# A two-layer graph attention kernel on one core: where the target's own row joins its early sums

## The chip, the cores and the metric

The kernel runs on one core of a Trainium2 chip. The metric is the device time of one execution in microseconds (us); lower is better. Three runs of the kernel before took 1847.95, 1852.89 and 1860.00 us, median 1852.89. The profile comes from one more execution.

## The reference, cut to what matters

There are 3327 nodes with 1024 features each and a symmetric 0/1 adjacency with self loops on the diagonal (each off-diagonal pair is an edge with a chance of about 0.5%). Two layers follow each other, each of the form `x = layernorm(x + attention(x))`.

```python
# layer 0: 8 heads of 128 features
h = (x @ W).reshape(C, H, D)
e = leaky(alpha_src[:, :, None] + alpha_dst[:, None, :], 0.2)   # per head, target i, source j
attn = softmax(where(adj == 0, -inf, e))
out = einsum('hij,hjd->hid', attn, h)
# layer 1: one head of 1024 features
h = x @ W;  e = leaky(h @ a1 + (h @ a2).T, 0.2)
out = relu(softmax(where(adj > 0, e, -9e15)) @ h)
```

Since exp is monotone, the kernel uses exp(leaky(s+d)) proportional to max(exp(0.8 s) exp(d), exp(0.2 d)) for a target with score s and a source with score d. A softmax is then a weighted sum of source rows over a sum of weights. The edge of a node to itself, its *own* edge, is kept out of the lists of edges and treated apart.

## The kernel before, in words

Rows come in NT = 26 tiles of P = 128 targets. A tile's edges lie in EB + 1 = 5 blocks: blocks 0 and 1 hold sources among the first 13 tiles (NTH = 13), 2 and 3 the rest, each as four groups of 128 source rows for 32 targets each, and block 4 is one group for what did not fit. Matmuls and the weights are fp32.

**Stage 1, projection (0 to about 570 us).** For each tile t, rows of x are loaded, turned by TensorE (L195), multiplied with the weights (`project`, L541, three column cuts of 346 or 347, eight matmuls each), taken out of PSUM by ScalarE (`keep`, L553) and stored to `h0_d` with exp(d) and exp(0.2 d) beside them. Masks of the adjacency are loaded by GpSimd's queue (`load_mask`, L527, three buffers), counted by ScalarE and packed by VectorE (`count`, `words`, L341), then made into edge lists in seven steps a tile (`listing`, L592), whose copies by ScalarE `mvg` (L449) wait for VectorE and GpSimd. The order on every engine is the order in which the program issues. `pace` (L629), called after every second matmul of `project`, moves three generators on: `counts` at every third call, `steps` so that 3/7 of the listing is done when tile 13 begins, and `soon`.

`soon` is `sums_so_far` (L646). It starts at t = 13 and gives, for the first EARLY = 17 targets' tiles, the sums over blocks 0 and 1 while the projection of the later tiles goes on. Per tile: `fetch` gathers four groups of source rows by GpSimd (three buffers, two blocks ahead), `weights` (L674) makes the matrix e on VectorE, `sums` (L686) does 16 matmuls for four heads into a PSUM tile `acc` of two banks, `den` sums the weights, ScalarE copies `acc` out to `z` (L738) and `den` to `dens` (L739), and `z` is stored to `half_d` (L740). There are nine yields a tile. The first matmul into each bank has `start`, so `acc` begins empty. What is left when the projection ends runs in one go (L925).

**Stage 2, layer 0 (about 575 to 1090 us).** `pipeline` (L1322) runs over 26 items `Layer0` (L1059): nine late tiles with five blocks, 17 early ones with blocks 2 to 4. For each, `prepare` (L1069) loads x, the tile's own rows with their two exponentials from `h0_d` (520 KB, `own`), and for an early tile also `half_d` (512 KB, `half`). `own` (L1080) makes the own weights es from `grows`, the loaded exponentials and `loop` (is there a self loop) on VectorE; `scale_own` (L1092) multiplies the own rows with es, eight ScalarE instructions; `sums` adds own (and half) to the accumulators by matmuls with the identity (L1128 to L1133). Gathers of source rows (L1036) use five buffers.

**Stage 3, layer 1 (about 1100 to 1777 us).** 26 items `Target` (L1199): gathers, sums (L1258) and a projection (L1290).

Of the kernel before, what the change touches and what calls it, by code (L numbers as in the profile page):

```python
# [9 lines left out]
F32 = mybir.dt.float32  # L10
# [16 lines left out]
def kernel(  # L27
# [102 lines left out]
    dens = const.tile([P, EARLY, H], F32, name="dens")  # L130
    io_t = const.tile([P, P], F32, name="io_t")

    near = [const.tile([P, NG, HG], F32, name=f"near{b}") for b in range(HB)]

# [377 lines left out]
    with ExitStack() as own, tc.manual_schedule():  # L512
# [14 lines left out]
        def load_mask(t):  # L527
            if t < NT:
                ads[t] = masks[t % 3]
                if t == NT - 1:  # L530
                    nc.vector.memset(ads[t].bitcast(I32), 0)
                    nc.vector.memset(ads[t][:, :1], 1.0)
                for r in pieces(t):
                    nc.gpsimd.dma_start(ads[t][r, :N], adj[at(t, r), :])
# [94 lines left out]
        def pace():  # L629

            slots[0] += 1
            n = slots[0]
            if n % 3 == 0:
                next(counts, None)
            first = 3 * total // 7
            if n <= turn_at[0]:
                aim = 4 + (first - 4) * n / turn_at[0]
            else:
                aim = first + (total - first) * (n - turn_at[0]) / (turn_at[1] - turn_at[0])
            while done[0] < aim:  # L640
                done[0] += 1
                next(steps, None)
            if soon:
                next(soon[0], None)

        def sums_so_far():  # L646
# [39 lines left out]
            def sums(acc, val, b, e, heads_):  # L686
                vals = val[:, :, :D].rearrange("p g (h d) -> p g h d", h=H)
                for h in heads_:
                    for g in range(NG):
                        nc.tensor.matmul(  # L690
                            acc[g * GT : (g + 1) * GT, h // 4, h % 4, :], e[:, g, h, :], vals[:, g, h, :],
                            start=b == 0 and h % 4 == 0, stop=b == HB - 1 and h % 4 == 3,
                        )
# [5 lines left out]

            res = [listed(0), listed(1)]  # L700
            for _ in range(3):
                yield
            for n in range(2):
# [5 lines left out]
            fetch(2)  # L709
            yield  # L710
            yield
            for s in range(EARLY):
                acc = part.bank("L", [P, 2, 4, DH], "part")
                made = []
                for b in range(HB):
                    n = s * HB + b
                    val = src[n % 3]
                    made.append(weights(val, b, res[0], oh))
                    yield
                    if n:  # L720
# [5 lines left out]
                    if b == 0:  # L726
                        yield
                        yield
# [7 lines left out]
                z = part.sbuf("z", [P, 2, 4, DH], 1)  # L736
                for n in range(2):
                    nc.scalar.activation(z[:, n], acc[:, n], AF.Copy)  # L738
                nc.scalar.activation(dens[:, s, :], den, AF.Copy)  # L739
                nc.sync.dma_start(half_d[s], z.rearrange("p n h d -> p (n h d)"))  # L740
# [5 lines left out]
                yield  # L746

# [19 lines left out]
        masks = [pool.tile([P, NP], U8, bufs=1, name=f"ad{n}") for n in range(3)]  # L767
# [107 lines left out]
        for t in range(3, NT):  # L875
# [3 lines left out]
            if t == 12:  # L879
# [11 lines left out]
            if t == 16:  # L891
# [80 lines left out]
    def sparse(own):  # L972
# [7 lines left out]
        grows = pool.tile([P, NT, H], F32, bufs=1, name="grows")  # L980
        nc.scalar.activation(grows, sd0[:, :, 0, :], AF.Exp, scale=1 - SLOPE)
# [77 lines left out]
        class Layer0:  # L1059
# [9 lines left out]
            def prepare(self):  # L1069
# [4 lines left out]
                self.h = sbuf("own", [P, HW0], 2)  # L1074
                nc.sync.dma_start(self.h, h0_d[self.t * P : (self.t + 1) * P, :HW0])
                if self.t < EARLY:
                    self.half = sbuf("xT", [P, KT, P], 2, "half").rearrange("p k q -> p (k q)")
                    nc.sync.dma_start(self.half, half_d[self.t])

            def own(self):  # L1080

                t, h = self.t, self.h
                es, total = sbuf("es0", [P, 2, H], 2).rearrange("p a h -> a p h")
                nc.vector.tensor_tensor(es, grows[:, t, :], h[:, D : D + H], OP.mult)
                nc.vector.tensor_tensor(es, es, h[:, D + H :], OP.max)
                nc.vector.tensor_scalar(es, es, loop[:, t : t + 1], None, op0=OP.mult)
                self.es = self.total = es
                if t < EARLY:
                    self.total = total
                    nc.vector.tensor_tensor(total, es, dens[:, t, :], OP.add)  # L1090

            def scale_own(self):  # L1092

                h = self.h
                for n in range(H):
                    d = slice(n * DH, (n + 1) * DH)
                    nc.scalar.activation(h[:, d], h[:, d], AF.Copy, scale=self.es[:, n : n + 1])  # L1097
# [25 lines left out]
            def sums(self, b):  # L1123
# [4 lines left out]
                if j in (1, 2):  # L1128
                    for rows_ in (self.h, self.half) if self.t < EARLY else (self.h,):
                        nc.tensor.matmul(  # L1130
                            self.acc[j - 1].rearrange("p h d -> p (h d)"), ident, rows_[:, (j - 1) * HALF : j * HALF],
                            start=False, stop=False,
                        )  # L1133
# [32 lines left out]
            def finish(self):  # L1166

                ri = sbuf("ri", [P, H], 2)
                nc.vector.tensor_tensor(ri, self.den, self.total, OP.add)
# [391 lines left out]
```

## Time and profile before

| what | value |
|---|---|
| median of 3 runs (lowest to highest) | 1852.89 us (1847.95 to 1860.00) |
| the profiled execution, its own time | 1778.88 us |
| its span, first to last instruction | 1777.1 us, mean granted TensorE clock 0.926 |
| TensorE busy over the span | 1518.3 us (85%) |
| VectorE, ScalarE, GpSimd busy | 1150.6, 537.5, 1111.7 us |
| moved by DMA | 592.41 MB, mean 333 GB/s |
| own<-h_d, 26 loads | 520.0 KB each |
| half<-half_d, 17 loads | 512.0 KB each |

The profiled execution was 74 us shorter than the median. A time and a difference read from the profile belong to that execution. "PE" is TensorE's matmuls, "PEld" its weight loads, "DVE" VectorE, "ACT" ScalarE, "POOL" GpSimd, "SP" the queue of SyncE, which issues most plain transfers. A wait is put down to the engine or transfer that came last. "DMA share" is the mean busy share of the 16 DMA engines in a window.

### The profile page before, as it was taken

How to read it: one execution, taken by the hardware profiler on the slowest of the kernel's cores; microseconds unless marked ns; L12 is line 12 of the kernel's file. 1: busy time of each engine (PE TensorE's matmuls, PEld its weight loads, DVE VectorE, ACT ScalarE, POOL GpSimd, SP SyncE). 2: the span in 40 equal slices, each digit the busy share in tenths (PEclk: the TensorE clock that was granted, in tenths of full speed). 3: DMA queues.
4: the chain of work that ended last, by engine and by line, in shares of the span. 5: the costliest groups of instructions: out<-in, count | busy, mean ns of one | idle time of the engine just before them, and what ended most of it. 6: DMA issues, size and time to landing. Idle time of an engine off the chain costs nothing.

```text
span 1777.1 us, 36731 instructions
## 1 busy us (share of the span) xinstructions
PE 1518.3 (85%) x13778; PEld 882.2 (50%) x13778; DVE 1150.6 (65%) x3125; ACT 537.5 (30%) x1602; POOL 1111.7 (63%) x1476
## 2 busy tenths in 40 slices
PE   8799999999995667666676674599999999999998
PEld 5466666666664455444554453244444444444443
DVE  6799999888873877767777775243444444444443
ACT  5678773333322233233333332011110111101110
POOL 4443358877755666656656666677676666676750
PEclk9999999999998788888788886899999999999999
DMA  7578978998888999999999999999999999999980
GB/s 195 100 138 167 163 170 302 319 314 319 296 303 331 407 411 408 394 384 406 395 397 393 385 402 365 355 395 403 396 393 386 394 390 396 401 401 395 386 345 36
DMA packets 189050, 592.41 MB, mean 333 GB/s; under 512 B 37069, under 2 KB 47079, under 8 KB 188864
## 3 DMA queue, kind: packets, MB, share of 16 engines
q0 software_dynamic: 131056, 458.88, 72.6%
q1 hardware_dynamic: 57650, 130.84, 19.8%
q8 instruction: 111, 1.82, 0.4%
q14 instruction: 75, 0.61, 0.1%
q10 hardware_dynamic: 158, 0.26, 0.0%
HBM read 590.02 MB, written 53.33 MB: 362 GB/s over the span
## 4 chain that ended last, share of the span: by engine, by line
PE 42%; DMA 18%; DVE 4%; issue 1%; ACT 1%; POOL 1%; DVEq 0%; SPq 0%; POOLq 0%; ACTq 0%
PE mm L1290 21%; PE acc L1258 13%; DMA src<-h_d,idx 7%; DMA own<-h_d 4%; PE acc L1147 3%; DMA near<-h_d,idx 3%; PE acc L1130 3%; DVE e L1115 2%; PE tr L195 1%; DMA src<-y_d,idx 1%; DMA near<-y_d,idx 1%; ACT own L1097 1%; DMA end<-h_d,idx 1%; DVE pr L1002 1%; PE acc L1138 1%
## 5 line engine op out<-in xcount | busy, mean ns | idle before, releaser
L545 PE MATMUL mm<-wt,xT 128*128 128x347 f32 (+1 forms) x1248 | 408.0, 468 | 2.1 <-DMA wt<-in_L_gnn_W_dram 1.5
L1290 PE MATMUL mm<-wt,xT 128*128 128x512 f32 x832 | 387.6, 604 | 0.0
L1036 POOL DMA_INDIRECT src<-y_d,idx x240 | 244.6, 1019 | 95.0 <-issue 32.7
L545 PEld LDWEIGHTS mm<-wt,xT 128*128 128x128 f32 x1248 | 225.7, 192 | 116.7 <-issue 18.4
L1036 POOL DMA_INDIRECT src<-h_d,idx x168 | 180.9, 1077 | 112.4 <-PE acc L1147 25.2
L1290 PEld LDWEIGHTS mm<-wt,xT 128*128 128x128 f32 x832 | 149.7, 189 | 199.1 <-issue 194.1
L1293 DVE SCALAR_TENSOR_TENSOR o<-mm,y 128x512 f32<-128x512 f32 x52 | 36.0, 692 | 317.1 <-PE mm L1290 317.1
L1036 POOL DMA_INDIRECT near<-y_d,idx x176 | 178.9, 1017 | 90.6 <-PE acc L1258 29.7
L1130 PE MATMUL acc<-own,ident 128*128 128x512 f32 x104 | 80.4, 865 | 118.8 <-ACT own L1097 115.2
L1036 POOL DMA_INDIRECT near<-h_d,idx x104 | 116.1, 1117 | 65.1 <-DMA src<-h_d,idx 13.9
L198 ACT ACTIVATE xT<-tr 128x512 f32<-128x512 f32 x104 | 63.2, 609 | 254.1 <-PE tr L195 254.0
L1272 ACT ACTIVATE z<-y,ri 128x342 f32<-128x342 f32 (+1 forms) x78 | 39.5, 569 | 300.5 <-DVE ri L1268 300.5
L660 POOL DMA_INDIRECT near<-h_d,idx x96 | 105.2, 1096 | 36.2 <-issue 24.4
L1120 ACT ACTIVATE w<-way 128x32 f32<-128x32 f32 (+1 forms) x96 | 18.5, 192 | 350.4 <-DVE e L1115 168.6
L1115 DVE TENSOR_TENSOR e<-oh,way 128x1024 f32<-128x1024 f32 x96 | 117.2, 1221 | 8.4 <-DVE way L1113 0.5
L1147 PE MATMUL acc<-src,e 128*32 128x128 f32 x2688 | 103.4, 318 | 17.6 <-DVE e L1115 17.6
L1258 PE MATMUL acc<-src,es 128*32 128x342 f32 (+1 forms) x1440 | 116.2, 454 | 0.2
L1258 PE MATMUL acc<-near,es 128*32 128x342 f32 (+1 forms) x1056 | 90.1, 476 | 28.0 <-DVE es L1249 28.0
L1147 PEld LDWEIGHTS acc<-src,e 128*32 128x32 f32 x2688 | 88.1, 129 | 47.1 <-DVE e L1115 31.9
L1147 PE MATMUL acc<-near,e 128*32 128x128 f32 x1792 | 65.8, 309 | 23.0 <-DVE e L1115 12.2
L348 ACT ACTIVATE junk<-ad 128x1664 uint8<-128x1664 uint8 x52 | 82.9, 1594 | 5.6 <-POOL ad L337 4.0
L1130 PEld LDWEIGHTS acc<-own,ident 128*128 128x128 f32 x104 | 20.4, 245 | 124.6 <-ACT own L1097 123.9
(238 smaller groups left out, 2577.8 us busy)
## 6 DMA issues: line engine op xcount, KB each, us to landing
own<-h_d SPq DMA_DIRECT2D x26, 520.0 KB
y_d<-y SPq DMA_DIRECT2D x26, 514.0 KB
y<-y_d SPq DMA_DIRECT2D x26, 514.0 KB
h_d<-ht SPq DMA_DIRECT2D x25, 520.0 KB
x<-in_x_dram SPq DMA_DIRECT2D x25, 512.0 KB
y<-in_x_dram SPq DMA_DIRECT2D x25, 512.0 KB
out_dram<-o SPq DMA_DIRECT2D x25, 512.0 KB
ad<-in_adj_dram POOLq DMA_DIRECT2D x25, 415.9 KB
```

The costliest lines, as they stand in the source:

```text
L198: nc.scalar.activation(part, tr, AF.Copy)
L348: nc.scalar.activation(junk, ad[:, n * THR : (n + 1) * THR], AF.Copy, accum_out=self.d[:, n : n + 1])
L545: nc.tensor.matmul(acc, xT[t][:, k, :], wt[:, k, CUTS0[c] : CUTS0[c + 1]], start=k == 0, stop=k == KT - 1)
L660: nc.gpsimd.indirect_dma_start(out=src[n % 3][:, g, :], out_offset=None, in_=h0_d[:THR, :], in_offset=bass.IndirectOffsetOnAxis(ap=idx[:, ...
L1036: nc.gpsimd.indirect_dma_start(out=s[:, g, :w], out_offset=None, in_=table[:n, :], in_offset=bass.IndirectOffsetOnAxis(ap=idx[:, t, b * NG ...
L1115: nc.vector.tensor_tensor(e, oh.unsqueeze(2).to_broadcast([P, ng, H, wide]), wp.unsqueeze(3).to_broadcast([P, ng, H, wide]), OP.mult,)
L1130: nc.tensor.matmul(self.acc[j - 1].rearrange("p h d -> p (h d)"), ident, rows_[:, (j - 1) * HALF : j * HALF], start=False, stop=False,)
L1147: nc.tensor.matmul(self.acc[h // 4][g * GT : (g + 1) * GT, h % 4, :], e[:, g, h, :], rowsof[:, g, h, :], start=first and h % 4 == 0, stop= ...
L1258: nc.tensor.matmul(self.acc[c][to, :m], es[:, g, :], s[:, g, CUTS[c] : CUTS[c + 1]], start=b == 0, stop=b == EB,)
L1272: nc.scalar.activation(z[:, cut], self.res[:, cut], AF.Copy, scale=ri[:, 1:2])
L1290: nc.tensor.matmul(acc, xT[:, k, :], wt1[:, k, half], start=k == 0, stop=k == KT - 1)
L1293: nc.vector.scalar_tensor_tensor(o[:, half], acc, 0.0, res[:, half], op0=OP.max, op1=OP.add)
```

## The change

- In `sums_so_far`, before the first sum of a tile, ScalarE writes the tile's own row, scaled by the own weight head by head, into `acc`: `lay` first has TensorE write zeros into a bank (one bf16 matmul of 512 columns with `start`), then ScalarE four times 128 columns. The sums have no `start` any more and so add to that. The row comes from `h0_d` by `own_row`, on SP's queue, into the storage of the masks, all of which must have been counted before (`need(NT - 2)`).
- The copy out of `acc` and its store are split into `settle(s, 0)` and `settle(s, 1)`; the second is issued in the first step of the next tile. The denominator is added to `own_e` by VectorE.
- `own_terms` makes the own weights for many tiles at once from the scores `sd0` (three Exp on ScalarE, three VectorE instructions): tiles 0 to 12 before the sums, 13 to 16 at s = 10, the nine late ones at the start of stage 2. `grows`, `dens`, the per-tile `own` arithmetic are gone.
- In layer 0 an early tile loads only `half_d`, into `own`; it has no scaling and one identity matmul per bank instead of two. A late tile loads 512 instead of 520 KB and scales as before.
- `pace` moves `counts` on at two of five calls instead of one of three, and `steps` so that 2/5 instead of 3/7 of the listing is done at tile 13. Masks rotate by one buffer; the diagonal of the adjacency is loaded at t = 5 instead of 12 and `loop` made at 11 instead of 16.

```diff
+    own_e = const.tile([P, NT, H], F32, name="own_e")
+    def own_terms(lo, hi, mids):
+        e, score = own_e[:, lo:hi, :], sd0[:, lo:hi, 1, :]
+        for mid, scale in zip(mids, (1.0, SLOPE)):
+            nc.scalar.activation(mid, score, AF.Exp, scale=scale)
+        nc.scalar.activation(e, sd0[:, lo:hi, 0, :], AF.Exp, scale=1 - SLOPE)
+        nc.vector.tensor_tensor(e, e, mids[0], OP.mult)
+        nc.vector.tensor_tensor(e, e, mids[1], OP.max)
+        nc.vector.tensor_tensor(e, e, loop[:, lo:hi].unsqueeze(2).to_broadcast([P, hi - lo, H]), OP.mult)
...
-                ads[t] = masks[t % 3]
+                ads[t] = masks[(t + 1) % 3]
...
-            if n % 3 == 0:
+            if n * 2 % 5 < 2:
                 next(counts, None)
-            first = 3 * total // 7
+            first = 2 * total // 5
...
-                            start=b == 0 and h % 4 == 0, stop=b == HB - 1 and h % 4 == 3,
+                            start=False, stop=b == HB - 1 and h % 4 == 3,
...
+            def own_row(s):
+                nc.sync.dma_start(row, h0_d[s * P : (s + 1) * P, :D])
+            def lay(s, n):
+                nc.tensor.matmul(
+                    acc[:, n], zeros, all_b.unsqueeze(1).to_broadcast([P, 4, P]), start=True, stop=False
+                )
+                for h in range(4 * n, 4 * n + 4):
+                    nc.scalar.activation(
+                        acc[:, n, h % 4, :], row[:, h * DH : (h + 1) * DH], AF.Copy, scale=own_e[:, s, h : h + 1]
+                    )
+            def settle(s, n):
+                if n == 0:
+                    zs.append(part.sbuf("z", [P, 2, 4, DH], 1))
+                nc.scalar.activation(zs[s][:, n], acc[:, n], AF.Copy)
+                if n == 1:
+                    nc.vector.tensor_tensor(own_e[:, s, :], own_e[:, s, :], den, OP.add)
+                    nc.sync.dma_start(half_d[s], zs[s].rearrange("p n h d -> p (n h d)"))
+            need(NT - 2)
+            row = ph.ads.rearrange("p a b -> p (a b)").bitcast(F32)[:, :D]
+            acc = part.bank("L", [P, 2, 4, DH], "part")
...
             for s in range(EARLY):
-                acc = part.bank("L", [P, 2, 4, DH], "part")
                 made = []
                 for b in range(HB):
                     n = s * HB + b
                     val = src[n % 3]
                     made.append(weights(val, b, res[0], oh))
+                    if b == 0 and s:
+                        settle(s - 1, 1)
+                        lay(s, 0)
                     yield
+                    if b == 0 and s:
+                        lay(s, 1)
                     if n:
                         fetch(n + 2)
                     yield
...
                     if b == 0:
                         yield
+                        if s + 1 < EARLY:
+                            own_row(s + 1)
...
-                z = part.sbuf("z", [P, 2, 4, DH], 1)
-                for n in range(2):
-                    nc.scalar.activation(z[:, n], acc[:, n], AF.Copy)
-                nc.scalar.activation(dens[:, s, :], den, AF.Copy)
-                nc.sync.dma_start(half_d[s], z.rearrange("p n h d -> p (n h d)"))
+                if s == EARLY - 1:
+                    yield
+                settle(s, 0)
...
             def prepare(self):
-                self.h = sbuf("own", [P, HW0], 2)
-                nc.sync.dma_start(self.h, h0_d[self.t * P : (self.t + 1) * P, :HW0])
-                if self.t < EARLY:
-                    self.half = sbuf("xT", [P, KT, P], 2, "half").rearrange("p k q -> p (k q)")
-                    nc.sync.dma_start(self.half, half_d[self.t])
+                self.h = sbuf("own", [P, D], 2)
+                h0 = h0_d[self.t * P : (self.t + 1) * P, :D]
+                nc.sync.dma_start(self.h, half_d[self.t] if self.t < EARLY else h0)
...
             def scale_own(self):
+                if t >= EARLY:
+                    for n in range(H):
+                        d = slice(n * DH, (n + 1) * DH)
+                        nc.scalar.activation(h[:, d], h[:, d], AF.Copy, scale=own_e[:, t, n : n + 1])
...
-                    for rows_ in (self.h, self.half) if self.t < EARLY else (self.h,):
-                        nc.tensor.matmul(
-                            self.acc[j - 1].rearrange("p h d -> p (h d)"), ident, rows_[:, (j - 1) * HALF : j * HALF],
-                            start=False, stop=False,
-                        )
+                    nc.tensor.matmul(
+                        self.acc[j - 1].rearrange("p h d -> p (h d)"), ident, self.h[:, (j - 1) * HALF : j * HALF],
+                        start=False, stop=False,
+                    )
```

## The prediction

> **What bounds the kernel now.** I read the page's slices first, to see that one number doesn't describe the whole span, then busy times by stretch.
>
> ```profile
> PE   8799999999995667666676674599999999999998
> DMA  7578978998888999999999999999999999999980
> GB/s 195 100 138 167 163 170 302 319 314 319 296 303 331 407 411 408 394 384 406 395 397 393 385 402 365 355 395 403 396 393 386 394 390 396 401 401 395 386 345 36
> ```
>
> ```profile
> core 0: us, PE busy (x) PEld busy (x) DVE busy (x) ACT busy (x) POOL busy (x), PEclk, DMA share, GB/s
> 75.00:252.00 177.00, 172.82 (x782) 113.89 (x780) 158.82 (x451) 137.06 (x385) 72.29 (x260) 1.00 0.85 152
> 252.00:570.00 318.00, 285.33 (x3373) 194.81 (x3372) 251.89 (x676) 109.20 (x412) 229.78 (x386) 0.97 0.88 309
> 575.00:1090.00 515.00, 348.30 (x5565) 252.77 (x5564) 383.48 (x955) 161.68 (x475) 328.32 (x303) 0.80 1.01 395
> 1100.00:1777.00 677.00, 644.24 (x3693) 276.88 (x3693) 291.39 (x867) 79.41 (x164) 435.56 (x429) 0.98 0.94 366
> ```
>
> Columns: stretch, length, busy time of each engine, TensorE's clock, DMA share, rate. The projection is TensorE's twice: 172.8 of 177 us, and with the early sums 285 of 318. Layer 0 belongs to the transfers: share 1.01 throughout, while no engine exceeds 383 of 515 us. Layer 1 is TensorE's and the change leaves it alone. Next, the transfers of layer 0 and its waits:
>
> ```profile
> q0 software_dynamic: 43391, 151.33, 74.8%
> q1 hardware_dynamic: 17317, 51.40, 25.9%
> ```
>
> ```profile
> PEld acc L1130 <- ACT own L1097: 123.9, 25, 14.1
> DVE es L1084 <- DMA own<-h_d: 46.1, 17, 13.2
> ```
>
> Packets, MB and share of 575 to 1090 us; then waits as sum, times, longest. TensorE stands 124 us behind the scaled own rows, a tempting number. But the transfer engines never rest meanwhile, so only removed bytes shorten this stage. Last, TensorE between two tiles of early sums, where the change puts its new work, and two ScalarE groups of 252 to 570 us:
>
> ```profile
> 389.54 0.29 PE L732 MATMUL dd<-w,oh 128*32 128x8 f32 x16
> 389.76 2.60 PE L545 MATMUL mm<-wt,xT 128*128 128x347 f32 x8
> ...
> 392.40 1.42 PE L545 MATMUL mm<-wt,xT 128*128 128x347 f32 x4
> 393.65 0.33 PE L468 MATMUL xp<-mvg,place 128*128 128x168 bf16 x3
> 395.14 1.08 PE L690 MATMUL part<-near,e 128*32 128x128 f32 x32 [1.16 <-issue]
> ```
>
> ```profile
> L449 ACT ACTIVATE mvg<-mvs,own_g 128x129 bf16<-128x129 bf16 x60 | 19.2, 395 | 39.9 <-POOL mvs L332 17.1 <-DVE mvs L438 14.2 <-DVE place L442 4.3
> L738 ACT ACTIVATE z<-part 128x512 f32<-128x512 f32 x34 | 18.5, 600 | 44.2 <-PE dd L732 25.1 <-PE part L690 12.9 <-issue 6.2
> ```
>
> From the end of one tile's denominator (389.8) to the next tile's first sum (395.1) TensorE has 5.3 us, 1.2 idle.
>
> **What the skill says.** The Trainium skill, "PSUM — Partial Sum Buffer", "The four PSUM rules", says that ScalarE's writes don't touch the bits by which a matmul adds or overwrites; hence the zero matmul ahead of each `lay`. Its section "PSUM bank collisions raise a hardware error" asks that accesses by two engines be ordered by bank. The instruction order of the changed kernel goes further, across both banks of the one tile: the second zero matmul of the first tile waits for ScalarE, though ScalarE touched only the other bank; a tile's first sum waits for ScalarE and its second half has no such wait, so the first covers both `lay`s; each of the four copies waits for the previous one. "DMA: Bandwidth & Descriptors", "Issuing engines are not separate DMA queues", says that transfers from SP and GpSimd share 16 engines; the trace agrees, their shares adding to 1.01.
>
> **The change, part by part.** The sum is made against the profiled execution (own time 1778.9, span 1777.1 us). The median is 74 us above it; I add differences to the median unscaled.
>
> *Layer 0, bytes.* 17 own loads of 520.0 KB go: 9.05 MB (KB of 1024 bytes). At 395 GB/s that is 22.9 us; by queue q1's own rate (25.9% of 515 us for 51.40 MB, 2.6 us a MB) 23.5. Nine late tiles save 8 KB each, 0.2 us. **-23 us.**
>
> *Layer 0, engines.* 34 identity matmuls of 0.87 us, 136 ScalarE copies (eight take 2.44 us in the timeline, 41 us in all), and three or four small VectorE instructions a tile (0.17 us each) go. Behind the transfers this is worth nothing; without that cover, 17/26 of the 124 us wait, 81 us, would be its ceiling. Bound from both sides: 0 by the share of 1.01, and if the rate rose to the best slices' 411 GB/s, (203.6 - 9.05)/0.411 = 473 us, 42 less than 515. I take 0 beyond the bytes and keep -42 as the far end.
>
> *Early sums, transfers.* 17 own rows of 512 KB move here on SP's queue, behind x loads, h stores and half stores; 8.9 MB at 2.6 us a MB, 23 us of DMA time. The stretch uses 0.88 of 318 us, 280, and then 303: 0.95. They fit if spread evenly. A row is issued five steps ahead, some 10 us; own rows are waited for up to 13 us in layer 0's full queues. Late rows would stop ScalarE, and behind it the h copies that the projection needs. Between 0 and 15 us; **+2**.
>
> *Early sums, the chain ahead of a tile's first sum.* Two copies out (L738, a pair takes 1.06 to 1.09 us), zero matmul, four copies, zero matmul, four copies. No trace row has ScalarE writing SBUF into PSUM; nearest is L1097, 0.388 us each, 0.305 apart when they overlap. Waiting for each other they don't, so 0.41; four are 1.6 us (bounds: 1.2 overlapped, 2 with slower hand-overs). A zero matmul of 512 bf16 columns: the skill's "TensorE: Matmul & The Clock Gate", "Back-to-back issue gap", states 518 cycles, 0.22 us at the full clock; L468's 168 columns take 0.24 with drain, so 0.25 to 0.3. With four hand-overs of some 0.1 us: 1.1 + 3.2 + 0.5 + 0.3 = 5.1 us. Into the same queue come ScalarE's other copies: (109.2 - 18.5)/318 = 0.29 of the time, 1.4 us; and `mvg` stands between a tile's first copy out and its last `lay` in about six of 17 tiles by the changed order, at 1.3 us plus its share of the 39.9 us waits (2.7 per listed tile, of which I count half): 6 x 2.6/17 = 0.9. Sum 7.4 against 5.3 now, +2.1 on 16 boundaries: 34 us. TensorE is idle 33 of 318 us; a later first sum gives VectorE and gathers time, whose waits (L690 stands 16.8 us behind DVE e, more on the weight loads) shrink; 10 us come back. **+24.** Bounds: +6 (chain in the idle time; bare zero matmuls) and +50 (nothing comes back, chain 8.5).
>
> *Tail.* The last two tiles have little projection to hide behind: the serial chain costs **+2**.
>
> *Stage 1 up to 252 us.* `counts` runs 6/5 as fast, the first-half listing shrinks from 80 to 74 steps. VectorE gets less before tile 13 and some 12 us more after: 252 + 12 of 318, still under TensorE. The transfer share 0.85 rises while masks last. The diagonal's load, 4.7 us on SP at L886, now stands ahead of x loads at t = 5, covered by their lead of three tiles. `own_terms` adds nine Exps in three calls and nine small VectorE instructions, `settle` 17 adds, minus `dens`'s 17 copies: 4 us on engines with room. 0, or up to +6 if a mask is late; the new `need` then stops the program at tile 13.
>
> Sum: -23 + 2 + 24 + 2 = +5 us, **1858 us**.
>
> **Rivals.**
> *The chain is hidden (faster).* For: TensorE's 33 us of idle time; ScalarE is 34% busy. Then stage 1 costs 3 us. Layer 0, with fewer separate loads and no own-row dependency for early tiles, runs at 400 GB/s: 194.6/0.400 = 486, 29 less. -26: **1827 us**. Against: the chain alone is 5.1 of 5.3 us, and in-order queues wait at its places.
> *The chain becomes the bound (slower).* Place: first sum of each tile, behind ScalarE. Price: 4 us a boundary, 64 us, 16 back, -23: +25, **1878 us**. It decides once a boundary grows by more than (23 + 18)/16 = 2.6 us net. For: `mvg`'s waits, reaching 4 us; the wait across both banks.
> *The transfer was hidden anyway.* If layer 0 had kept time by TensorE's own-row waits, losing them would bring more, not less; if by gathers' issue on GpSimd (328 of 515 us busy), nothing: 1853 + 28 = 1881. The share of 1.01 speaks against it.
> *The change doesn't do what it says.* Bytes might merely move between two full stages; the projection's 0.88 speaks against that, and the time would again be about 1876.
>
> **How the numbers follow.** 1% (18.5 us) is about what a measurement of this kernel can tell from no change. Likeliest, 0.46: layer 0 gives 23 and early sums take about as much; own range 1838 to 1871. Hidden chain, 0.24, around 1827: faster by over 1%. Chain, late rows, late masks, or hidden transfers, 0.30 together, around 1878: slower by over 1%. The 8-in-10 range leaves out half of the faster case's far side and the slow one's: 1827 to 1886.
>
> **What would show it.** Layer 0 still at share 1.0 and about 195 MB, shorter by 23 us: right. The stretch from tile 13 to the last half store longer by about 28 us, with TensorE's weight loads or matmuls at the zero matmul and first sum waiting for ScalarE: right; no such waits, the first rival. ScalarE waiting for the own row: transfers too slow. A share much below 1 in layer 0 would upset the byte sum, and a pause at 250 us would put the loss on the masks.

## The result and the profile after

The changed kernel takes 1899.22 us (median of 4 runs, 1897.00 to 1907.72); the kernel before, run beside it, 1851.19 us (1847.95 to 1860.00). The ratio is 1.026, 95% interval 1.021 to 1.031: slower, by about 48 us where 5 were forecast. The profiled execution of the changed kernel took 1900.04 us, with a span of 1898.3 us, so this time the profile and the median agree.

One thing has to be said ahead of all that follows: the chips were met in two conditions. In one the unchanged kernel before takes about 1780 us (the profile shown ahead of the prediction, and experiments e1 to e8), in the other about 1855 us (the three times ahead of the prediction, the comparison above, and e9 to e15). I call them the 1780 and the 1855 condition. The record gives the same chip number for e5 to e8, which met the first, and for e12 to e15, which met the second. So the profile of before shown ahead of the prediction and the profile of after come from different conditions, and a before from each (e1, e9) is needed to read them.

The slices of the page of the kernel after:

```profile
PE   8799998888788568777778877499999999999998
...
GB/s 183 95 135 165 193 219 259 267 287 254 238 293 275 304 376 377 368 319 393 384 336 369 386 361 384 306 359 388 380 387 371 385 375 380 394 390 384 367 360 34
```

Slices 7 to 13, the early sums, show TensorE at 7 to 8 tenths where the earlier profile had mostly 9. Slices 15 to 25, layer 0, show a rate of 319 to 393 GB/s; in the earlier profile layer 0 lies in slices 14 to 24 and has 384 to 411. Now busy time by stretch: first the kernel after in the 1855 condition (the profile of the comparison), then the kernel before in that condition (e9), then the kernel after in the 1780 condition (e5). Columns as in the prediction: stretch, length, busy time of TensorE, its weight loads, VectorE, ScalarE and GpSimd, TensorE's clock, DMA share, GB/s. In each, the first line is the early sums and the second is layer 0.

```profile
252.00:640.00 388.00, 321.46 (x3434) 210.32 (x3435) 267.28 (x735) 159.85 (x559) 221.68 (x403) 0.95 0.79 273
645.00:1195.00 550.00, 419.69 (x5629) 278.93 (x5630) 374.89 (x885) 128.24 (x350) 335.88 (x315) 0.84 0.96 366
```

```profile
252.00:595.00 343.00, 308.38 (x3365) 203.46 (x3363) 254.44 (x684) 111.22 (x421) 220.96 (x386) 0.97 0.81 279
600.00:1158.00 558.00, 427.92 (x5717) 277.29 (x5718) 391.45 (x977) 165.78 (x484) 333.63 (x316) 0.84 0.99 380
```

```profile
252.00:600.00 348.00, 305.38 (x3372) 203.78 (x3370) 267.35 (x737) 160.23 (x565) 222.54 (x401) 0.97 0.84 300
605.00:1110.00 505.00, 325.35 (x5595) 251.57 (x5599) 373.17 (x883) 123.74 (x344) 330.18 (x308) 0.79 1.01 392
```

The reader is to see two things. In the 1780 condition the change did to layer 0 what was forecast: the share stays at 1.01, and the stage takes 505 us where before had 528 there (e1: 568 to 1096 us). In the 1855 condition TensorE is busy in layer 0 for 428 us before and 420 us after, where it needs 352 (e1) and 325 (e5) in the other condition for about the same number of matmuls, and the share falls to 0.96 once the bytes are gone. Transfers are no longer what this stage waits for most. The chain of waits, followed back from the end, says the same: over layer 0 of the kernel before it lies on transfers for more than half of the time in e1 (`src` gathers 25.6%, `near` gathers 12.9%, own rows 12.8%, `end` gathers 4.0%), but in e9 mainly on TensorE's matmuls into the accumulators (L1147 30.7%, L1130 13.5%) and on pauses that the profile puts down to nothing (19.8%). The largest waits of the kernel after in layer 0 (sum, times, longest):

```profile
PEld acc L1190 <- issue: 204.6, 324, 11.7
...
PE acc L1190 <- issue: 96.7, 253, 1.1
```

The wait for the scaled own rows that led this list before (124 us in the profile ahead of the prediction) is gone from the top; in its place stand pauses that the profile puts down to nothing, marked "issue". In the kernel before in the same condition they lead already (e9, the same view; L1147 is the same line there):

```profile
PEld acc L1147 <- issue: 163.7, 252, 11.3
```

In the 1780 condition it is small (e1, 568 to 1096 us):

```profile
PEld acc L1147 <- issue: 20.5, 7, 11.5
```

Last, the place where the prediction put its chain: TensorE between two tiles in the kernel after, and ScalarE beside it. This boundary is one of the short ones, 5.9 us; the mean is 8.8.

```profile
337.13 0.35 PE L787 MATMUL dd<-w,oh 128*32 128x8 f32 x16
...
338.67 0.38 PE L719 MATMUL part<-all_b,zeros 128*128 128x512 bf16 x1
338.89 1.33 PE L555 MATMUL mm<-wt,xT 128*128 128x347 f32 x4
340.72 0.38 PE L719 MATMUL part<-all_b,zeros 128*128 128x512 bf16 x1 [0.50 <-ACT part L723]
340.94 1.33 PE L555 MATMUL mm<-wt,xT 128*128 128x347 f32 x4
343.39 1.08 PE L700 MATMUL part<-far,e 128*32 128x128 f32 x32 [1.13 <-ACT part L723]
```

```profile
337.50 1.09 ACT L730 ACTIVATE z<-part 128x512 f32<-128x512 f32 x2 [2.96 <-issue]
339.09 1.58 ACT L723 ACTIVATE part<-ad,own_e 128x128 f32<-128x128 f32 x4 [0.50 <-PE part L719]
340.61 1.26 ACT L459 ACTIVATE mvg<-mvs,own_g 128x129 bf16<-128x129 bf16 x4
341.78 1.56 ACT L723 ACTIVATE part<-ad,own_e 128x128 f32<-128x128 f32 x4
```

Everything stands in the forecast order: both copies out, zeros, four own copies (1.58 us; 1.6 were forecast), `mvg` in between, zeros, four copies, and only then, at 343.39, the first sum. These are TensorE's waits there over the early sums (252 to 640 us) in the kernel after; in the kernel before (e1, e9) the sums show no wait for the copies out, and ScalarE writes nothing into the accumulators:

```profile
PE part L719 <- ACT z L730: 28.0, 12, 4.7
...
PEld part L700 <- ACT part L723: 24.4, 16, 4.0
...
PE part L700 <- ACT part L723: 14.4, 13, 2.5
```

From the start times of single rows I made a table of stages in us. "Early sums end" is the start of the last copy out of `acc`; "layer 0" runs from there to the start of its last block-4 matmul; "boundary" is the mean over the 16 tile changes of the time from the end of a tile's denominator to the next tile's first sum, as in the prediction.

| run | kernel | condition | early sums end | layer 0 | boundary |
|---|---|---|---|---|---|
| e1 | before | 1780 | 565.9 | 533.2 | 4.6 |
| e5 | after | 1780 | 603.3 | 509.9 | 7.1 |
| e3 | after, two accumulators | 1780 | 575.9 | 508.5 | 5.0 |
| e7 | after, no own row | 1780 | 575.2 | 509.1 | 4.5 |
| e8 | after, own row loaded but unused | 1780 | 575.1 | 508.3 | 4.7 |
| e9 | before | 1855 | 598.2 | 561.8 | 4.7 |
| e15 | after | 1855 | 644.3 | 552.6 | 8.9 |
| e11 | after, two accumulators, two stores | 1855 | 622.3 | 550.6 | 5.9 |
| e12 | before, fewer bytes | 1855 | 602.5 | 552.0 | 4.7 |
| e13 | after, no own row | 1855 | 605.9 | 551.6 | 4.7 |

Layer 1 (first to last projection matmul) takes 622 us in the first condition and 644 to 645 in the second, in both kernels.

### The profile page after: what moved, and what is told of

Read it like the earlier page. It is cut to its first block, busy times and chain, and to the rows that moved or that the text cites. A ratio compares the mean times of both kernels' runs of the same rounds, so it can differ in the third digit from the quotient of the medians.

```text
span 1898.3 us, 36583 instructions
## 1 busy us (share of the span) xinstructions
PE 1635.8 (86%) x13744; PEld 927.4 (49%) x13744; DVE 1136.4 (60%) x3057; ACT 549.1 (29%) x1593; POOL 1089.6 (57%) x1476
## 4 chain that ended last, share of the span: by engine, by line
PE 55%; issue 7%; DVE 2%; DMA 1%; POOL 0%; DVEq 0%; POOLq 0%; ACT 0%; ACTq 0%
PE mm L1333 20%; PE acc L1301 14%; PE acc L1190 12%; PE acc L1181 4%; PE acc L1173 3%; PE tr L205 1%; DVE pr L1056 1%; PE den L1201 1%; DMA av<-in_L_gnn_a_dram 0%; DMA near<-y_d,idx 0%; DMA src<-y_d,idx 0%; PE tr L1237 0%; DVE e L1159 0%; POOL near L1090 0%; PE den L1185 0%
## 5 line engine op out<-in xcount | busy, mean ns | idle before, releaser
L555 PE MATMUL mm<-wt,xT 128*128 128x347 f32 (+1 forms) x1248 | 422.0, 478 | 3.3 <-DMA wt<-in_L_gnn_W_dram 2.9
L555 PEld LDWEIGHTS mm<-wt,xT 128*128 128x128 f32 x1248 | 232.8, 197 | 155.5 <-issue 62.4
L1333 PEld LDWEIGHTS mm<-wt,xT 128*128 128x128 f32 x832 | 149.6, 189 | 200.6 <-issue 195.6
L1190 PE MATMUL acc<-src,e 128*32 128x128 f32 x2688 | 149.4, 295 | 56.9 <-issue 53.2
L1190 PE MATMUL acc<-near,e 128*32 128x128 f32 x1792 | 108.9, 298 | 58.1 <-issue 44.8
L1190 PEld LDWEIGHTS acc<-src,e 128*32 128x32 f32 x2688 | 92.3, 117 | 119.1 <-issue 104.4
L1090 POOL DMA_INDIRECT near<-h_d,idx x104 | 111.3, 1070 | 58.3 <-issue 19.0
L1301 PE MATMUL acc<-src,es 128*32 128x342 f32 (+1 forms) x1440 | 126.4, 455 | 3.5 <-issue 1.8
L670 POOL DMA_INDIRECT near<-h_d,idx x96 | 102.5, 1067 | 43.9 <-issue 24.9
L1301 PE MATMUL acc<-near,es 128*32 128x342 f32 (+1 forms) x1056 | 97.1, 468 | 25.6 <-DVE es L1292 22.5
L1190 PEld LDWEIGHTS acc<-near,e 128*32 128x32 f32 x1792 | 64.6, 117 | 105.8 <-issue 101.4
L1164 ACT ACTIVATE w<-way 128x32 f32<-128x32 f32 (+1 forms) x96 | 18.2, 190 | 268.6 <-DVE e L1159 160.4
L1181 PEld LDWEIGHTS acc<-end,e 128*128 128x128 f32 x416 | 77.2, 279 | 15.9 <-issue 11.4
```

Source lines behind the costliest of these rows:

```text
L555: nc.tensor.matmul(acc, xT[t][:, k, :], wt[:, k, CUTS0[c] : CUTS0[c + 1]], start=k == 0, stop=k == KT - 1)
L670: nc.gpsimd.indirect_dma_start(out=src[n % 3][:, g, :], out_offset=None, in_=h0_d[:THR, :], in_offset=bass.IndirectOffsetOnAxis(ap=idx[:, ...
L1090: nc.gpsimd.indirect_dma_start(out=s[:, g, :w], out_offset=None, in_=table[:n, :], in_offset=bass.IndirectOffsetOnAxis(ap=idx[:, t, b * NG ...
L1181: nc.tensor.matmul(self.acc[h // 4][:, h % 4, :], e[:, 0, h, :], rowsof[:, 0, h, :], start=False, stop=h % 4 == 3,)
L1190: nc.tensor.matmul(self.acc[h // 4][g * GT : (g + 1) * GT, h % 4, :], e[:, g, h, :], rowsof[:, g, h, :], start=first and h % 4 == 0, stop= ...
L1301: nc.tensor.matmul(self.acc[c][to, :m], es[:, g, :], s[:, g, CUTS[c] : CUTS[c + 1]], start=b == 0, stop=b == EB,)
```

## The experiments

My theory after the result: the chain behind ScalarE at each tile change is the loss, and it is as long as it is because both banks are one tile of the program, so that each step waits for the other bank too. The rivals are the store of `z` (one buffer, its second half copied only when the next tile has begun), the own rows' transfers, and that the difference of 48 us is one of chips. The runs of one group below were measured beside one another, and beside the kernel before.

**e1, e2, e3, e4: one group, 1780 condition.** e1 is the kernel before, unchanged.

> The kernel before, unchanged, profiled once more. The profile of the kernel after shows three stretches longer than that of before: the stretch of early sums (252 us to the last copy out of the accumulators) by 78 us, layer 0 not shorter, layer 1 by 23 us, though the change doesn't touch layer 1; its records have pauses before TensorE's weight loads that are put down to nothing ('issue'). Theory A, the execution and not the change made part of this: a second profile of before gives about 1850 us, with early sums ending near 580 us, layer 0 near 540 us long and layer 1 some 20 us longer than in the first, and the pauses are in it. Theory B, the change made all of it: about 1779 us again, with the same stretches as in the first profile and no such pauses.

Measured: 1779.87 us, ratio 0.9987 to the kernel before in the same group (0.9974 to 1.0000; the 95% interval stands in brackets from here on), span 1777.5 us. The profile ahead of the prediction was no accident of one execution: this condition comes back, and holds for a whole group of runs.

e2 gives each half of `z` a buffer and a store of its own (tile 0's turned rows move to make room):

```diff
-                xT[t] = ph.sbuf("xT", [P, KT, P], 2) if t else part.sbuf("z", [P, KT, P], 1, "xT")
+                xT[t] = ph.sbuf("xT", [P, KT, P], 2) if t else far[:, 1, :D].rearrange("p (k q) -> p k q", q=P)
...
-                if n == 0:
-                    zs.append(part.sbuf("z", [P, 2, 4, DH], 1))
-                nc.scalar.activation(zs[s][:, n], acc[:, n], AF.Copy)
+                z = part.sbuf("z", [P, 4, DH], 2)
+                nc.scalar.activation(z, acc[:, n], AF.Copy)
...
-                    nc.sync.dma_start(half_d[s], zs[s].rearrange("p n h d -> p (n h d)"))
+                nc.sync.dma_start(half_d[s][:, n * HALF : (n + 1) * HALF], z.rearrange("p h d -> p (h d)"))
```

> The kernel after, but each half of a tile's early sums is copied out to a buffer of its own (two half buffers in the room of one) and stored at once, so that the first copy of the next tile no longer waits for a store that was issued only one step into that tile. Theory 'store': in the profile of after the copies out wait 30 us for something without a name, 7 times, and the event waits before them have a median of 3.3 us; this is the store of the tile before, and TensorE's 28 us wait for the copies follows from it. Then this runs about 25 to 30 us faster than after, near 1872. Theory 'chain': the order of zero matmul, copies, zero matmul, copies across both banks is what TensorE waits for; then it gains under 8 us, above 1890.

Measured: 1795.35 us, ratio 1.0078 (1.0062 to 1.0095). The kernel after itself has 1.0067 (1.0043 to 1.0090) in this condition (e5), which is the same within the intervals. The theory of the store falls.

e3 makes the two banks two tiles and leaves all else (the places that name `acc` change with it):

```diff
-            part.more_banks(own, "part", {"L": 1})
+            part.more_banks(own, "part", {"L": 2})
...
-            acc = part.bank("L", [P, 2, 4, DH], "part")
+            acc = [part.bank("L", [P, 4, DH], "part") for _ in range(2)]
```

> The kernel after, but the accumulator of the early sums is two tiles of one bank each, so that the second zero matmul doesn't wait for ScalarE's writes to the first bank, and the first sum only for those to its own bank. Theory 'chain': of the some 60 us that TensorE stands in the early sums behind ScalarE (28 behind the copies out, 9 at the zero matmuls and about 24 at the first sums behind the own rows), the last two shrink to a few us: about 25 us faster than after, near 1874. Theory 'store': under 8 us, above 1890.

Measured: 1765.67 us, ratio 0.9915 (0.9893 to 0.9936). The same work, and 30 us less than e2 beside it, which has the kernel after's time. One of its tile changes:

```profile
306.52 0.29 PE L787 MATMUL dd<-w,oh 128*32 128x8 f32 x16
...
308.01 0.38 PE L719 MATMUL part<-all_b,zeros 128*128 128x512 bf16 x1
...
309.40 0.38 PE L719 MATMUL part<-all_b,zeros 128*128 128x512 bf16 x1
...
310.87 1.08 PE L700 MATMUL part<-near,e 128*32 128x128 f32 x32
```

From 306.81 to 310.87, 4.1 us, and no matmul in it shows a wait for ScalarE; over all early sums its row `PEld part L700 <- ACT part L723` falls to 11.7 us (25.9 in e5). So the order by bank that the Trainium skill asks for ("PSUM — Partial Sum Buffer", "PSUM bank collisions raise a hardware error") is enough here, and in this condition the wait across banks was the cost. e4 has both edits:

> Both edits together, two stores and two accumulators. If the two waits are separate, the gains add: some 50 us faster than after, near 1848, about the time before, since layer 0 has lost its bytes but zero matmuls and own copies stay. If the two are one queue seen at two places, it gains no more than the better of the two alone (1872 or so). If it ends clearly under 1840, the bytes saved in layer 0 show.

Measured: 1764.96 us, ratio 0.9902 (0.9882 to 0.9922): the same as e3 within the intervals, and a shorter time than both kernels have in this condition.

**e5, e6, e7, e8: one group, 1780 condition, to take the sum apart.** e5 is the kernel after, unchanged.

> The kernel after, unchanged, beside the kernel before on one chip. The second profile of before showed that the first one was no accident: 1777.5 us, the same stretches; so the chips differ (before took 1851 on one and 1782 on another). Theory 'the change alone': the ratio stays at 1.026, some 1828 us where before takes 1782; layer 0 is about 24 us shorter than before's and layer 1 equal, and the early sums take all of the loss, ending 70 us later than 566. The pauses without a name of the first profile of after (89 us before TensorE's sums in layer 0) are then absent. Rival, the change brings the pauses: they are here again, and layer 0 isn't shorter.

Measured: 1794.21 us, ratio 1.0067 (1.0043 to 1.0090), before 1780.86. e6 is the kernel before in which an early tile loads no own row in layer 0. It also scales nothing and has one identity matmul a bank instead of two there, and so leaves out the early tiles' own edge:

```diff
                 self.h = sbuf("own", [P, HW0], 2)
-                nc.sync.dma_start(self.h, h0_d[self.t * P : (self.t + 1) * P, :HW0])
                 if self.t < EARLY:
-                    self.half = sbuf("xT", [P, KT, P], 2, "half").rearrange("p k q -> p (k q)")
-                    nc.sync.dma_start(self.half, half_d[self.t])
+                    nc.sync.dma_start(self.h[:, :D], half_d[self.t])
+                else:
+                    nc.sync.dma_start(self.h, h0_d[self.t * P : (self.t + 1) * P, :HW0])
...
```

> The kernel before with one edit in layer 0: an early tile loads only its half sums and not its own row, adds only these with one identity matmul per bank, and scales nothing. It leaves out the own edge of the early tiles, in sums and denominators. This is layer 0's part of the change by itself. Theory 'bytes': 9.05 MB at 395 GB/s, 23 us less: ratio 0.987. Theory 'waits': if TensorE's 124 us behind the scaled own rows set the pace, up to 81 us less, ratio 0.955. Theory 'hidden': no change, 1.00.

Measured: 1760.75 us, ratio 0.9874 (0.9844 to 0.9904), 20 us less by the medians of this group, 22 by the ratio, where 23 were forecast for the bytes. The bytes and the work on the engines go together here and weren't told apart; the sum of both is no more than the bytes were to bring. e7 is the kernel after without zeros, own rows and own copies in the early sums, so it leaves out the own edge as well:

```diff
-                            start=False, stop=b == HB - 1 and h % 4 == 3,
+                            start=b == 0 and h % 4 == 0, stop=b == HB - 1 and h % 4 == 3,
...
-            own_row(0)
...
-            lay(0, 0)
...
-                        lay(s, 0)
...
-                        lay(s, 1)
...
-                        if s + 1 < EARLY:
-                            own_row(s + 1)
```

> The kernel after without zero matmuls, own rows and own copies in the early sums; the first sum of a bank starts it, as before. It leaves out the own edge of the early tiles in the sums. Kept are the split copies out, the store that is issued a step later, the pacing and the masks read by tile 12, and layer 0's saving. If these are harmless, it takes the time of the bytes alone (0.987). If the late store and the wait across both banks cost without any own row, it is slower, up to 1.005.

Measured: 1763.22 us, ratio 0.9895 (0.9875 to 0.9915). So splitting the copies out and the new pacing cost 2.5 us over e6, which is within the intervals. e8 is e7 with the own rows loaded and unused (the two `own_row` calls put back):

> As the one before, but the own rows are loaded in the early sums and used by nobody: the price of their transfers alone. The prediction gave 2 us (0 to 15) for them: ratio within 0.002 of the kernel without them. If the transfers of the early sums are as full as their share of 0.88 lets fear, 15 us or 0.008 more.

Measured: 1766.18 us, ratio 0.9908 (0.9886 to 0.9930). The rows cost 3.0 us, again within the intervals. From e8 to e5 are 28.0 us, the chain; e3, which has all of it but the wait across banks, stands at e8's ratio.

**e9, e10, e11: one group, 1855 condition.** e9 is the kernel before, e10 the kernel after, both unchanged, e11 is e4 again.

> The kernel before again, in the hope of a chip like that of the first comparison, where before took 1851 us. There the profile of after has some 70 pauses a 100 us before TensorE's weight loads in layer 0 (40 us in 100, put down to nothing), where the later profile of after has 4, and its chain of waits in layer 0 is TensorE's, not the transfers'. If the chip is of that kind and the pauses are its own, they are in this kernel too, layer 0 takes about 545 us here as well, and TensorE carries it. If they come with the change, they are absent here. If the chip takes 1781 us, this tells nothing new.

> The kernel after on the same chip. On a chip of the first kind: ratio 1.026 as at first, with layer 0 about as long as before's, since where TensorE carries layer 0, fewer bytes save nothing and only 34 identity matmuls go; the early sums then make the loss of some 50 us. On a chip of the second kind: 1.007 again.

> The version with two accumulators and two stores on the same chip. On a chip of the second kind 0.990 again. On one of the first kind the saved bytes don't show and the chain is mended: 0.995 to 1.005.

Measured: e9 1860.24 us, ratio 0.9991 (0.9970 to 1.0011); e10 1895.43 (two runs only, 1887.85 and 1903.01), 1.0196 (1.0134 to 1.0257), before 1861.17; e11 1876.94, 1.0095 (1.0069 to 1.0121). e10 is slower than before, but by less than the 1.026 that I expected, which lies just beyond its interval. e11 missed what I expected of it: the version that gains 1% in one condition loses 1% in the other. Layer 0 gains only 11 us in e11 (550.6 against 561.8) and the early sums end 24 us later, not 7. The wait across banks costs there as well (e11 is 18.5 us below e10), but it isn't all: e13 below, without any own row, has a ratio of 0.9998, so the chain with two tiles, its rows included, still costs about 18 us in this condition (an estimate from the two ratios).

**e12, e13, e14, e15: one group, 1855 condition.** e12 is e6 and e13 is e7 again, e15 the kernel after.

> Before, with early tiles loading only their half sums in layer 0 (it leaves out their own edge in sums and denominators), a second time, in the hope of a chip on which before takes about 1855 us. Theory 'TensorE carries layer 0 there': on such a chip the bytes give what layer 0 gave in the kernel after, 9 to 12 us: 1843 to 1847 of 1855, ratio 0.993 to 0.996. Theory 'bytes are worth as much everywhere, and the kernel after loses them elsewhere': 22 us, ratio 0.988. On a chip on which before takes about 1781 it repeats 0.987.

Measured: 1855.59 us, ratio 0.9986 (0.9971 to 1.0001), before 1857.47. Less than either theory gave: layer 0's part of the change brings 2 us. In the table layer 0 is 10 us shorter than in e9 and the early sums end 4 us later. But e9 is from another group, in which the kernel before took 4 us more, so stages of different groups agree only to some us, and for the whole time the medians of one group decide. That layer 0 itself is 9 to 11 us shorter than e9's holds for e11, e12, e13 and e15 alike; why so little of it is left in e12's time isn't resolved.

> After without zero matmuls, own rows and own copies in the early sums (it leaves out their own edge in the sums), a second time. On a chip on which before takes about 1855 us the early sums of the kernel after end 44 to 50 us later than before's. Theory 'the chain costs more there': nearly all of it goes with the chain, the early sums end within 10 us of before's and the ratio is 0.993 to 1.0. Rival 'splitting the copies out and the new pacing cost there': the early sums still end 20 us or more later, and the ratio is 1.005 or more. On a chip on which before takes about 1781 it repeats 0.99.

Measured: 1855.95 us, ratio 0.9998 (0.9984 to 1.0012). The early sums end at 605.9, 8 us after before's and 38 before those of the kernel after: nearly all of the delay goes with the chain, here too.

e14 asks what TensorE's pauses in layer 0 come from. It is the kernel after, but gathers only one group of four there once a buffer has been filled, so it leaves out the right rows for the other three:

```diff
+            whole = w != HW0 or k not in filled
+            if not end:
+                filled.add(k)
-            for g in range(NG if b < EB else 1):
+            for g in range(NG if b < EB and whole else 1):
```

> After, with three of four gathers of layer 0 left out once each buffer has been filled (sums of layer 0 then use rows that are not theirs). Transfers of layer 0 fall from about 200 to some 85 MB. On a chip of about 1781: if transfers carry layer 0, its stretch falls from 510 us to what TensorE's 325 us and its waits need, 380 to 430 us, time 1680 to 1720. On a chip of about 1855: if TensorE's pauses of 0.3 us come from contention with the transfers, they vanish and layer 0 takes the same 380 to 430 us there; if they are TensorE's own or its instruction supply's, the pauses stay, and layer 0 stays at 520 us or more.

> The kernel after, unchanged, for the same chip as the three others: 1.02 to 1.026 where before takes about 1855 us, 1.007 where it takes about 1781.

Measured: e14 1765.99 us, ratio 0.950 (0.947 to 0.953); e15 1896.16, 1.0206 (1.0175 to 1.0238). Both kernels have the same matmuls. The timeline of TensorE in the same stretch, first in e15:

```profile
906.12 0.46 PE L1190 MATMUL acc<-near,e 128*32 128x128 f32 x4 [0.29 <-issue]
906.84 0.43 PE L1190 MATMUL acc<-near,e 128*32 128x128 f32 x5 [0.27 <-issue]
```

and in e14, which has one whole block of the same line in one piece:

```profile
901.45 1.95 PE L1194 MATMUL acc<-near,e 128*32 128x128 f32 x64
```

Four records and a pause of 0.3 us, again and again, against 64 in 1.95 us (each fp32 matmul of the program stands as two records). Over layer 0 the row of pauses falls from the first of these in e15 (650 to 1195 us) to the second in e14 (655 to 1065 us):

```profile
PEld acc L1190 <- issue: 202.5, 317, 11.4
```

```profile
PEld acc L1194 <- issue: 45.6, 60, 10.8
```

Layer 0 takes 418.5 us where e15 has 552.6, and its DMA share is 0.72 (0.97 in e15). So with three of four gathers gone, most of the pauses go too. It isn't shown that TensorE pauses just when the transfers are dense. Taken in pieces of 10 us, e15's layer 0 has more pauses where the share is below 0.95 (7 for every 64 weight loads) than where it is 1.0 or more (3), and pieces with a share of 0.7 to 0.85 have 6 in e15 but under 1 in e14. Nor do the pauses fall at random: counted by blocks of 64 weight loads, the blocks with six or more pauses in e15 have 6.5 on the mean in e10, which ran under another chip number, and those with at most two have 1.8.

What TensorE waits for stays open. That it is the supply of instructions is a guess that no run here tests: the expectation of e14 counted it among the causes whose pauses would stay, but a supply that the traffic slows would recover with fewer transfers. The instruction transfers that the profile lists (q8) are the same 46 in layer 0 of e5 and e15 and take 0.6% and 0.5% of the DMA engines' time, so they are not slower, but whether they come late isn't shown. ScalarE too has such pauses there in e15 (before `w`, L1164, 80.4 us in 25 waits; in e5 that row is missing). And e14 also takes away three of four of GpSimd's gather instructions, so the traffic and the making of it weren't told apart. Why a chip is in one condition or the other is open as well.

## Why the prediction was wrong

**Layer 0, bytes, -23: right where it was read, wrong where it was used.** e6 measures 20 to 22 us and e5's layer 0 is 23.3 us shorter than e1's, in the 1780 condition, whose profile I had. The time I forecast was a median of the 1855 condition, and there layer 0's part alone brings 1.9 us (e12). This is the step that failed: "only removed bytes shorten this stage" was read from a profile 74 us below the median, and "I add differences to the median unscaled" carried it over. Those 74 us were no noise spread over the span. Of the 83 us between the spans of e9 and e1, the early sums hold 32, layer 0 29 and layer 1 about 22, and in layer 0 they replace the bound: transfers in e1, TensorE with its pauses in e9. The saved transfers shorten what mostly no longer ends last. The same carrying over made the chain too small, as the paragraph on it shows.

**Layer 0, engines, 0.** Right in the 1780 condition: the share stayed at 1.01, and of the 81 us of waits behind own rows nothing shows beyond what the bytes were to bring. In the other, identity matmuls and scalings go from a stage that TensorE bounds, and all together the stage gains 9 us (e15).

**Early sums, transfers, +2.** Measured 3.0 in the 1780 condition (e8 over e7), which is within the intervals. No wait of ScalarE for the own row is among the waits of the kernel after.

**The chain, +24, bounds +6 and +50: right mechanism, near in size only in the 1780 condition.** There the time grows by 28.0 us from e8 to e5. The mean boundary grows from 4.7 us (e8) to 7.1, 2.4 more where 2.1 were forecast, or 38 us for 16 of them; the early sums end 28 us later, so 10 us came back inside the tiles, as forecast. That the boundary grew from 5.3 to 7.4 was read from a single one; the mean before is 4.6. (The working also put four hand-overs of 0.1 us at 0.3.) In the 1855 condition a boundary grows by 4.2 us, from 4.7 (e13) to 8.9 (e15), 68 us in all; the early sums end 38 us later, so 29 came back, and chain and rows are worth 40.2 us of the time. So the term that was mis-sized is the boundary, twice as long there as forecast. Why it grows more there isn't shown.

Four own copies measured 1.58 us. The zero matmuls have rows of 0.38 us, but the next matmul starts 0.22 us after each (338.67 to 338.89, 340.72 to 340.94), the figure that the Trainium skill gives ("TensorE: Matmul & The Clock Gate", "Back-to-back issue gap"). The reading of the instruction order, waits across both banks, named the whole cost in the 1780 condition: with two tiles (e3) the boundary is 5.0 us and the chain costs nothing that shows. In the 1855 condition it is about half of it: with two tiles (e11) the boundary is 5.9 us, and some 18 us stay.

**Tail +2, stage 1 0.** Stage 1 is right: TensorE has 172.0 us of work between 75 and 252 us in the kernel after and 172.8 before, with no pause at 250 us. The tail wasn't taken apart.

**The sums.** In the 1780 condition: bytes -20, pacing and split copies +2.5, rows +3, chain +28: +13.4 us, against +5 forecast. In the 1855 condition: bytes -1.9, pacing and split copies +0.4 (e13 over e12), chain with rows +40.2: +38.7 us, e15's distance to before. Each sum comes out by itself, since its terms are differences of neighbouring runs. The first comparison gave +48 (ratio 1.021 to 1.031, e15 1.0175 to 1.0238); what the other 9 us are wasn't taken apart. Against the forecast, the bytes are off by 21 us and the chain with its rows by 14.

**The rivals.** "The chain becomes the bound" described what happened: it put the place, the mechanism and 4 us a boundary, and stopped at 1878 because it too deducted the 23 us of bytes. "The transfer was hidden anyway" gave 1881 and named TensorE or GpSimd's issue as what would hide it; the share of 1.01 spoke against it, and in the condition of the median that share is 0.99 with TensorE as the bound. Each of the two was half of it; I held them as alternatives, and the case in which both are true, 1853 + 40, had no chance of its own. "The chain is hidden" is refuted by the waits for ScalarE. "The change doesn't do what it says", bytes moved from one full stage to another, is refuted in the 1780 condition by the 3 us that the rows cost in their new place (e8); in the other the rows weren't run alone.

## What to carry to other kernels

When the profiled execution differs from the median by several per cent, ask first whether both were measured in the same condition: a bound read from the one need not be the bound of the other, and a saving in a stage with two nearly equal bounds is worth its size only where that one ends last. When a second engine is given writes into an accumulator, make each bank a tile of its own, and look in the instruction order for waits across banks: here that alone was 30 us of 1795. Price a chain at a tile change from the mean over all tile changes, not from one, and check what the tiles give back: here 10 of 38 us.

## What the runs showed of the hardware that I had not expected

- Under one chip number the same program ran at 1781 us in one group of runs and at 1857 in another, each steady within 1%. TensorE's granted clock over the span was 0.934 in e9, not lower than the 0.926 of the first profile.
- In the slower of the two, layer 0's streams of small fp32 matmuls (32 weight columns, 128 columns moved) often pause about 0.3 us after three to five records; a block of 64 records takes 1.95 us without pauses. With three of four gathers left out, and the DMA share of the stage down from 0.97 to 0.72, they are mostly gone. Stage 1 between 75 and 252 us, with the projection's larger matmuls, shows nothing of it: TensorE is busy 172.5 us in e1 and 172.6 in e9.
- ScalarE writing 128 columns of SBUF into PSUM, scaled, one copy waiting for the other, takes four in 1.58 us.
